# Two layers of a sequence model on one core: the Wo product in one piece, another order of the first loads, new costs in the planner, a longer ring of weights

## The chip, the cores and the metric

The kernel runs on one core of a Trainium2 chip. A core has five engines that work side by side, each with its own queue of instructions that it takes strictly in order: TensorE (PE in the profile; its weight loads are listed apart as PEld), VectorE (DVE), ScalarE (ACT), GpSimd (POOL) and SyncE (SP), which here issues transfers only. Engines wait for each other by semaphores. Transfers (DMA) run on 16 DMA engines; a queue of SP, ACT or POOL starts them. The metric is the device time of one execution in microseconds (us), lower is better; it is given as the median of several executions.

## What is computed

Two layers over 2 sequences of 1024 tokens with 512 features, all in float32. Each sub-layer is followed by a residual sum and a layer norm ("post-norm"). Cut to what matters:

```
x = layernorm(x + attn(x))        # A: q,k,v = silu(x Wq), silu(x Wk), silu(x Wv), 16 heads of 32
                                  #    chunks of 128 tokens: scores = (q k^T) * D, state S carried on with decay
                                  #    o = rms_norm_per_head(o * sigmoid(x Wg1 Wg2)) * w ;  out = o Wo
x = layernorm(x + ffn0(x))        # F: h = silu(x W1^T) * (x W3^T) ; out = hadamard(h) W2^T, 2048 wide
x = layernorm(x + scan(x))        # S: delta = softplus(...); h_t = exp(delta A) h_{t-1} + (delta x) B_t
                                  #    y = sum over 32 states of h_t C_t, + x D
x = layernorm(x + ffn1(x))        # f: h = silu(x Wg^T) * (x Wu^T) ; out = h Wd^T, 2048 wide
```

The Hadamard transform is applied to W2 once, at the start, instead of to the hidden values.

## The kernel before

**Groups and phases.** The tokens are cut into five groups (line 38): group 0 has the first two chunks of 128 tokens of the first sequence, group 1 four chunks of the second, group 2 four of the first, group 3 the last four of the second, group 4 the last two of the first. Each group g goes through V (values), A (attention), F (first feed-forward), the scan, and f (second feed-forward). `PHASES` (line 41) lists them in the order V0 A0 V1 A1 F0 F1 V2 A2 f0 F2 V3 A3 a1 F3 V4 A4 b1 F4 f2 f3 f4. Four of them are fillers (line 43): F0, f0, and the halves a1 and b1 of f1. Their matmuls have no hurry and are there to be put between the short, dependent steps of the attention of another group: F0 beside A1, f0 beside A2, a1 beside A3, b1 beside A4. The scan of a group runs on ACT (exponentials), POOL (products and sums) and DVE (the scan itself) beside the matmuls of later phases.

**The planner.** The order of instructions isn't written out by hand. Each step is an `Op` (line 68) with an engine, an estimated cost in us, a priority, the buffers that it reads, writes, takes and frees. `Order.run` (line 163) plays the whole program against these costs while the kernel is built: of the ops whose inputs are there, each engine's best is the one that can start at once, by priority, else the one that can start first; the earliest of these is put. The order in which ops are put is the order in which the engines execute them, so costs decide the order, not the time. `begin` (line 105) says when an op can start: the engine is free, inputs are written, and buffers of a named kind (`tags`) are free. With `spare` an op starts only if one buffer more than it needs is free; the fillers f0, a1 and b1 use it for their first matmuls (lines 1057 and 1108).

**Costs.** `mm_us`, `dve`, `act` and `pool` (lines 269 to 282) give a cost from the number of columns; some ops have their own (the moments of a norm at 555, `scaled` at 944, the state scan at 1436).

**Accumulators.** Matmuls write to four banks of 128x512 float32 with the tag `mm` (line 233). Every product takes one, a score step takes two at once (line 838), and the bank is free again when DVE or ACT has read it.

**Attention.** `attention` (line 612) runs the projections, then for each block of heads: transposed and decayed keys, state updates, gate, scores (two pairs of heads), outputs, then `gated`, a norm over each head (`norm`, 923) and `scaled` (938), after which the block's `normed` is set. `mixes` (981) is the product with Wo. A chunk takes four matmuls into one bank: the first two need only the first half of the blocks, the last two the second half. The list on line 984 puts the first halves of chunks 0 and 1 ahead, so that two banks are held from then until the last blocks are normed. `mixed` adds the residual and the norm, `turn` (507) transposes the result for F.

**Weights.** `load_weights` (346) streams pieces of 128x512 (256 KB) on SP through a ring of 12 buffers (`RING`, line 34), in the order of `PLAN`. At the start it holds after 4 pieces (wv) until two of the four quarters of W2 are issued, and after 12 (wq, wk) until all four are. `transformed_w2` (1138) loads the quarters (1 MB each); `butterflies` (DVE) and `w2_products` (PE, ACT) transform them and store them. `load_first` (408) loads the identity, the tokens of group 0 and the 64 KB Hadamard matrix. `load_others` (378) loads the tokens of later groups, those of group 1 at once. `load_consts` (421) loads the small tensors that the gate and the decays need.

**Scan sums.** `sums` (1464) adds the 64 partial results of a scan, every other one by an accumulating DMA. The four transposes per chunk that follow (`outputs`, 1499) are planned 6 us after the last sum (line 1493), to leave time for the last of these transfers.

Of the kernel before, what the change touches and what calls it, by code (L numbers as in the profile page):

```python
# [30 lines left out]
)  # L31


RING = 12
DB = 5
HPB = P // HD

# [41 lines left out]
class Order:  # L79
# [22 lines left out]
    def spawn(self, gen, prio=0):  # L102
        self.new.append([gen, prio, None])

    def begin(self, op):

        t = self.free[op.eng]
        for b in op.r:
            if b.written is None:
                return None  # L110
            t = max(t, b.written + self.HOP)
        for b in op.w:
            t = max(t, b.last + self.HOP)
        for name in {name for name, _ in op.a}:
            n, _, bufs = self.tags[name]
            k = sum(name == v for v, _ in op.a) + op.spare - (n - len(bufs))
            if k > 0:
                free = sorted(b.last for b in bufs if b.refs <= 0)
                if len(free) < k:
                    return None  # L120
                t = max(t, free[k - 1] + self.HOP)
        return t
# [40 lines left out]
    def run(self):  # L163
        while True:
            while self.new:
                th = self.new.pop(0)
                if self.advance(th):
                    self.threads.append(th)
            best = {}
            moved = False  # L170
            for th in list(self.threads):
                op = th[2]
                if not isinstance(op, Op):
                    if op():
                        moved = True
                        if not self.advance(th):
                            self.threads.remove(th)
                    continue
                t = self.begin(op)
                if t is None:  # L180
                    continue
                prio = op.prio + th[1]
                wrong = self.switches(op)
                now = t <= self.free[op.eng]
                key = (0, prio, wrong, t) if now else (1, t, prio, wrong)
                if op.eng not in best or key < best[op.eng][0]:
                    best[op.eng] = (key, t, th)
            if moved or self.new:
                continue
            if not best:  # L190
                assert not self.threads, [
                    (th[0].__name__, getattr(th[2], "eng", None)) for th in self.threads
                ]
                return
            _, t, th = min(best.values(), key=lambda v: v[1])
            self.put(th[2], t)
            if not self.advance(th):
                self.threads.remove(th)
# [3 lines left out]
def two_layers(  # L202
# [64 lines left out]


    def mm_us(n, cols):
        return n * max(cols * 4 / 2400 + 0.006, 0.28 if cols <= P else 0)  # L270

    def pe(us, fn, **kw):
        return Op("PE", us, fn, **kw)

    def dve(cols, fn, **kw):
        return Op("DVE", 0.145 + cols * 1.05e-3, fn, **kw)

    def act(cols, fn, **kw):
        return Op("ACT", 0.18 + cols * 0.81e-3, fn, **kw)

    def pool(cols, fn, **kw):
        return Op("POOL", 0.15 + cols * 2.25e-3, fn, **kw)

    def dma(nbytes, dst, src, eng="SP", **kw):
        of = {"SP": nc.sync, "ACT": nc.scalar, "POOL": nc.gpsimd}[eng]
# [59 lines left out]

    def load_weights():
        for i, (src, b, needs) in enumerate(pieces):
            if i in (EB, 3 * EB):
                Pools.w = i
                yield lambda: Pools.w2 >= i // EB // 3 * 2 + 2  # L350
            yield dma(
                KB256, lambda: b.t if len(src.shape) == 2 else b.t.rearrange(
                    "p (k c) -> p k c", k=2
                ), lambda: src, a=[("w", b)], r=needs,
            )
# [22 lines left out]
    def load_others():  # L378
        for gi in range(1, len(GROUPS)):
            yield gate_before(max(PHASES.index(f"V{gi}") - 1, 0))  # L380
            yield from load_x(gi)

    cst = cp.tile([P, 2 * P + 5], F32, name="cst")
# [24 lines left out]
    def load_first():  # L408
        nc.vector.memset(one, 1.0)
        nc.vector.memset(eps, EPS)  # L410
        nc.vector.memset(eps4, 4.0 * EPS)
        yield dma(KB256 / 4, lambda: ident, lambda: consts[:, C_ID : C_ID + P], w=[ident_b])
        yield from load_x(0)
        yield dma(
            65536, lambda: early[:, 0, :], lambda: consts[:, C_H : C_H + P], w=[hadamard_b]
        )
        spawn(load_weights())
        spawn(transformed_w2())
        spawn(load_consts())
# [112 lines left out]
    def normalized(gi, c, stage, store=None):  # L532

        xb = xn[gi, c]
        mv = sm.tile([P, nc.vector.BN_AGGR_DIM], F32, name="mv")
        rstd = sm.tile([P, 1], F32, name="rstd")
        neg = sm.tile([P, 1], F32, name="neg")
        nmr = sm.tile([P, 1], F32, name="nmr")
        stats = sm.tile([P, nc.vector.BN_STATS_DIM], F32, name="stats")
        s = Buf()  # L540

        def moments():
            nc.vector.bn_stats(stats, xb.t)
            nc.vector.bn_aggr(mv, stats)
            nc.vector.tensor_scalar_mul(neg, mv[:, 0:1], -1.0)

        def scales():
            log_tables()
            nc.scalar.activation(rstd, mv[:, 1:2], AF.Ln, bias=eps)
            nc.scalar.activation(rstd, rstd, AF.Exp, scale=-0.5)  # L550
            nc.scalar.activation(nmr, neg, AF.Copy, scale=rstd)
            nc.scalar.activation(xb.t, xb.t, AF.Identity, bias=nmr, scale=rstd)

        urgent = -2 if store is None else 0.2
        yield Op("DVE", 0.95, moments, w=[xb, s], prio=urgent)
        yield Op(
            "ACT", 1.6, scales, r=[s],
            w=[xb] if store is not None else [xb, there[gi, c, stage]], table=LOG, prio=urgent,
        )
        if store is not None:  # L560
            r0 = store + c * P
            yield dma(
                KB256, lambda: out[r0 : r0 + P, :], lambda: xb.t, eng="ACT", r=[xb], free=[xb]
            )
# [47 lines left out]
    def attention(gi, nxt, prio):  # L612
# [95 lines left out]
        def block(vb):  # L708
# [211 lines left out]
            def norm():  # L920
# [15 lines left out]
                def scaled():  # L936
# [4 lines left out]
                        )  # L941

                yield Op(
                    "DVE", 0.2 * S + 0.55, scaled, r=[sg, oT.whole], w=[parts[vb]], free=[sg]
                )
                normed[vb].written = parts[vb].written

# [31 lines left out]
            attended.add(gi)  # L979

        def mixes():
            accs = {}
            half = VB // 2
            for c, k in [(0, 0), (1, 0), (0, 1), (1, 1), (2, 0), (2, 1), (3, 0), (3, 1)][: 2 * n]:
                if True:
                    def mm(k=k, c=c):
                        for k_ in range(2 * k, 2 * k + 2):
                            nc.tensor.matmul(  # L988
                                accs[c].t, oT.t[:, k_, c * P : (c + 1) * P], w_o[k_].t,
                                start=k_ == 0, stop=k_ == EB - 1,  # L990
                            )

                    need = [oT.whole] + normed[k * half : (k + 1) * half]
                    ws = w_o[2 * k : 2 * k + 2]
                    if k == 0:
                        accs[c] = Buf()
                    yield pe(
                        mm_us(2, 512), mm, r=need + ws, a=[] if k else [("mm", accs[c])],
                        w=[accs[c]] if k else [],
                        free=(ws + ([oT.whole] if k else [])) if c == n - 1 else [],  # L1000
                    )
                if k:
                    spawn(mixed(c, accs[c]))

        def mixed(c, bank):
            xb = xn[gi, c]
# [14 lines left out]
    def ffn(ph, xT, store, prio=0):  # L1021
# [5 lines left out]
        for fh, nt in enumerate(parts):  # L1027
# [65 lines left out]
            def sums_of(c, f0):  # L1093
# [10 lines left out]
                if f0 == 0:  # L1104
                    accs[c] = Buf()
                yield pe(
                    mm_us(4, 512), mm, r=hs + ws, a=[] if f0 else [("mm", accs[c])],
                    spare=ph in FILLERS and ph != "F0" and f0 == 0,
                    w=[accs[c]] if f0 else [], free=hs + ws if c == n - 1 else [],
                )  # L1110

# [26 lines left out]
    def transformed_w2():  # L1138
        for dq in range(4):
            f, b = Buf(), Buf()  # L1140
            cols = slice(dq * q_d, (dq + 1) * q_d)
            if dq == 2:
                yield lambda: Pools.w >= 3 * EB
            yield dma(
                4 * KB256, lambda: f.t, lambda: w2t[:, cols].rearrange("(c p) d -> p c d", p=P),
                a=[("w2f", f)],
# [56 lines left out]
    class Scan:  # L1203
# [83 lines left out]
        def softplus(self, k, bank, u):  # L1287
# [11 lines left out]
            def logs():  # L1299
# [11 lines left out]
                prio=late,  # L1311
            )
            yield dve(
                T, lambda: nc.vector.tensor_add(r.t[:, :T], a.t[:, :T], r.t[:, :T]),
                r=[a], w=[r], free=[a], prio=late,
            )
            yield dma(
# [75 lines left out]
        def decays(self):  # L1393
# [3 lines left out]
            for i, (n, k0) in enumerate(self.units):  # L1397
                da, delta = self.da[i], self.delta[k0 // self.W]
                for j in range(self.W):
                    def exp():  # L1400
# [3 lines left out]
                            scale=a_s[:, k0 + j, n : n + 1],  # L1404
                        )

                    yield act(
                        self.T, exp, r=[delta, scan_b] + ([da] if j else []),
                        a=[] if j else [("da", da)],
                        free=[delta] if i + len(self.delta) >= U and j == self.W - 1 else [],  # L1410
                        table=EXP,
# [6 lines left out]
        def steps(self):  # L1418
# [3 lines left out]
            for i, (n, k0) in enumerate(units):  # L1422
                da, db, cs = self.da[i], self.db[i], self.cs[i // 2]
                d = lambda: da.t.rearrange("p a (r t) -> p (a r) t", r=self.R)
                for j in range(self.W):
                    def scan():
# [6 lines left out]
                        )  # L1433

                    yield Op(
                        "DVE", 0.145 + T * 2.15e-3, scan, r=[self.dec[i, j], db, da],
                        w=[self.scanned[i]], prio=1,
                    )
                if not ends(gi):
# [24 lines left out]
        def sums(self):  # L1464
# [25 lines left out]
                    r=[ys[1]], w=[ys[0]], free=[ys[1]],  # L1490
                )

            self.summed.written = max(y.written for y in ys) + 6.0
            self.done = True
            spawn(self.outputs())

# [153 lines left out]
```

## Time and profile before

| What | Value |
|---|---|
| Device time, median of 3 (lowest to highest) | 1854.84 us (1851.3 to 1860.04) |
| The profiled execution: its time, and the span from its first to its last instruction | 1854.81 us, 1853.0 us |
| PE busy | 1778.2 us, 96% |
| DVE busy | 1313.0 us, 71% |
| ACT busy | 1148.7 us, 62% |
| POOL busy | 1070.0 us, 58% |
| Mean granted TensorE clock | 0.985 of full speed |
| One 128x128 by 128x512 float32 product, shown as two records | 0.858 us start to start in a dense stretch (8 records in 3.43 us) |

"Busy" of an engine is the time in which it had an instruction; a low clock makes PE look busy for longer. So what is lost on PE is its idle time and, beside it, the time in which the granted clock was below 1. In a table by windows each row is a stretch of the span: its length, the busy us (and instructions) of each engine, the granted clock, the share of the DMA engines and GB/s. In a timeline a row is a run of equal instructions: start, length, engine, line, what it writes and reads, count, and in brackets the idle time before it and what ended that.

### The profile page before, as it was taken

The page shows a single profiled execution, that of the slowest core. Times are in us where ns is not written, and L with a number is a line of the kernel's source. Part 1 is how long each engine was busy: PE and PEld are TensorE (multiplying, and loading weights), DVE is VectorE, ACT ScalarE, POOL GpSimd, SP SyncE. Part 2 cuts the span into 40 slices and gives each one's busy share as a digit, 9 for nine tenths or more (in the row PEclk, how much of TensorE's full clock was granted, in tenths as well). Part 3 has the DMA queues.
Part 4 walks back from the last instruction along what each step waited for, and adds up shares of the span by engine and source line. Part 5 has one row for each costly group of instructions (what it writes and reads, how often), then busy time and mean ns, then how long its engine had stood idle before and what let it go on. Part 6 is the DMA issues. An engine that isn't in the chain of part 4 may idle for free.

```text
span 1853.0 us, 21250 instructions
## 1 busy us (share of the span) xinstructions
PE 1778.2 (96%) x7064; PEld 1006.8 (54%) x7064; DVE 1313.0 (71%) x1557; ACT 1148.7 (62%) x1820; POOL 1070.0 (58%) x558
## 2 busy tenths in 40 slices
PE   7999999999979999999899999999999899999998
PEld 3557754444555744444567444577775344544574
DVE  6431138994689989923999999549998998998211
ACT  3552058687756776757677757677676858775221
POOL 0000027884487899813778989337899877786000
PEclk9999999999989999999899999999999999999999
DMA  9524455774747978725478887487998775676252
GB/s 261 180 65 129 136 161 143 192 187 122 228 103 199 266 198 229 204 91 187 116 215 247 215 221 203 118 250 226 263 257 235 186 199 170 185 179 165 74 171 84
DMA packets 227708, 336.32 MB, mean 181 GB/s; under 512 B 21264, under 2 KB 131216, under 8 KB 227600
## 3 DMA queue, kind: packets, MB, share of 16 engines
q1 hardware_dynamic: 209024, 271.53, 46.8%
q0 software_dynamic: 16272, 59.25, 17.0%
q10 hardware_dynamic: 2304, 4.20, 0.6%
q8 instruction: 56, 0.92, 0.2%
q14 instruction: 52, 0.43, 0.1%
HBM read 253.12 MB, written 22.54 MB: 149 GB/s over the span
## 4 chain that ended last, share of the span: by engine, by line
PE 73%; DVE 10%; DMA 6%; ACT 5%; issue 3%; POOL 2%; SPq 0%; DVEq 0%; POOLq 0%; ACTq 0%
PE mm L1043 37%; PE mm L1097 20%; PE mm L645 5%; DVE da L1430 5%; DMA y<-dbu 3%; PE mm L594 2%; PE mm L988 2%; POOL dbu L1382 1%; ACT da L1402 1%; PE mm L832 1%; PE mm L514 1%; DVE dbu L1443 1%; DMA w<-in_wgut_dram 1%; PE mm L1244 1%; ACT L488 1%
## 5 line engine op out<-in xcount | busy, mean ns | idle before, releaser
L1382 POOL TENSOR_TENSOR dbu<-du,B 128x1024 f32<-128x1024 f32 x256 | 651.7, 2558 | 149.4 <-DMA y<-dbu 108.9
L1043 PE MATMUL mm<-xT,w 128*128 128x512 f32 (+1 forms) x1912 | 667.9, 510 | 3.6 <-DVE h L1074 1.7
L1043 PEld LDWEIGHTS mm<-xT,w 128*128 128x128 f32 x1912 | 363.3, 190 | 307.5 <-issue 269.6
L1402 ACT ACTIVATE da<-delta,a_s 128x512 f32<-128x512 f32 (+1 forms) x640 | 384.5, 605 | 148.2 <-DVE dbu L1443 121.5
L1430 DVE TENSOR_TENSOR_SCAN da<-da,hlast,dbu 128x512 f32<-128x512 f32 (+1 forms) x384 | 425.7, 1109 | 37.2 <-ACT da L1402 21.3
L1479 POOL TENSOR_TENSOR y<-y,dbu 128x1024 f32<-128x1024 f32 x123 | 323.1, 2627 | 49.7 <-DVE dbu L1443 42.9
L1097 PE MATMUL mm<-w,h 128*128 128x512 f32 x768 | 337.7, 595 | 7.5 <-DVE h L1074 4.5
L1443 DVE TENSOR_TENSOR dbu<-da,C 128x1024 f32<-128x1024 f32 x256 | 312.9, 1222 | 13.8 <-ACT hlast L1455 6.8
L1430 DVE TENSOR_TENSOR_SCAN da<-da,dbu 128x256 f32<-128x256 f32 (+1 forms) x256 | 245.9, 961 | 20.3 <-ACT da L1402 11.0
L1097 PEld LDWEIGHTS mm<-w,h 128*128 128x128 f32 x768 | 145.0, 191 | 181.9 <-issue 166.6
L1043 PE MATMUL mm<-xf,w 128*128 128x256 f32 x1024 | 230.3, 384 | 3.8 <-ACT hf L488 2.1
L1043 PEld LDWEIGHTS mm<-xf,w 128*128 128x128 f32 x1024 | 195.2, 192 | 39.3 <-issue 4.8
L488 ACT ACT_TABLE_LOAD x141 | 180.9, 1283 | 9.0 <-PE mm L645 3.8
L488 ACT ACTIVATE h<-mm 128x512 f32<-128x512 f32 x144 | 85.8, 597 | 128.9 <-PE mm L1043 64.9
L1402 ACT ACT_TABLE_LOAD x107 | 137.3, 1283 | 1.9
L1074 DVE TENSOR_TENSOR h<-h,mm 128x512 f32<-128x512 f32 x96 | 65.2, 679 | 90.3 <-PE mm L1043 84.5
L1455 ACT COPY hlast<-da 128x2 f32<-128x2 f32 (+1 forms) x160 | 25.4, 158 | 165.7 <-DVE dbu L1443 146.5
L735 POOL TENSOR_TENSOR qd<-h,q_dec 128x512 f32<-128x512 f32 x14 | 18.2, 1297 | 184.1 <-ACT h L488 118.6
L645 PE MATMUL mm<-xT,w 128*128 128x512 f32 (+1 forms) x320 | 118.3, 519 | 5.2 <-DVE sc L850 2.9
L288 POOL DMA_DIRECT2D y<-dbu x113 | 109.3, 967 | 11.5 <-DMA y<-dbu 6.6
L1116 DVE TENSOR_TENSOR xn<-mm,xn 128x512 f32<-128x512 f32 x60 | 41.0, 683 | 105.2 <-PE mm L1097 105.2
L1097 PE MATMUL mm<-w,hf 128*128 128x512 f32 x256 | 112.2, 592 | 0.0
(95 smaller groups left out, 1356.7 us busy)
## 6 DMA issues: line engine op xcount, KB each, us to landing
y<-dbu POOLq DMA_DIRECT2D x113, 512.0 KB, 6.2
w<-in_wgut_dram SPq DMA_DIRECT2D x192, 256.0 KB, 4.5
B<-rows SPq DMA_DIRECT2D x128, 256.0 KB, 4.6
C<-rows SPq DMA_DIRECT2D x128, 256.0 KB, 4.5
w<-in_wdnt_dram SPq DMA_DIRECT2D x96, 256.0 KB, 4.8
w<-in_w1t_dram SPq DMA_DIRECT2D x80, 256.0 KB, 4.4
w<-in_w3t_dram SPq DMA_DIRECT2D x80, 256.0 KB, 5.1
w<-w2h SPq DMA_DIRECT2D x80, 256.0 KB, 4.6
```

Of the source, the lines that this page charges most:

```text
L288: return Op(eng, us, lambda: of.dma_start(dst(), src(), **more), dma=nbytes, **kw)
L488: nc.scalar.activation(dst, src, AF.Silu)
L645: nc.tensor.matmul(bank.t[:, s * T : (s + 1) * T], w_qk[j][k].t[:, eb * P : (eb + 1) * P], xT.t[:, k, :], start=k == 0, stop=k == EB - 1,)
L1043: nc.tensor.matmul(bank.t[:, s * T + c0 * P : s * T + c1 * P], blocks[fb // 2][j][k // 2].t[:, k % 2 * 2 * P + k0 : k % 2 * 2 * P + k0 + P ...
L1074: 512, lambda: nc.vector.tensor_mul(t.t, t.t, pu.t), r=[pu], w=[t], free=[pu]
L1097: nc.tensor.matmul(accs[c].t, hT[f // S].t[:, s * T + c * P : s * T + (c + 1) * P], w_d[f].t, start=f == 0, stop=f == nt * S - 1,)
L1116: nc.vector.tensor_add(xb.t, bank.t, xb.t)
L1382: 1024, lambda: nc.gpsimd.tensor_mul(self.wide(self.db[i]), self.wide(du), self.row(self.bs, i)),
L1402: nc.scalar.activation(d[:, j, :], self.wide(delta)[:, j, :], AF.Exp, scale=a_s[:, k0 + j, n : n + 1],)
L1430: nc.vector.tensor_tensor_scan(d()[:, j, :], d()[:, j, :], self.wide(db)[:, j, :], init, ALU.mult, ALU.add,)
L1443: 1024, lambda: nc.vector.tensor_mul(self.wide(db), d(), self.row(self.cs, i)),
L1479: 1024, lambda: nc.gpsimd.tensor_add(y.t, y.t, db[i].t), r=o, w=[y],
```

## The change

It has seven parts.

- `mixes`: one op per chunk with all four matmuls, after every block is normed. No bank is held by a half product.
- The planner: if the best op for PE can't start, or starts more than 1 us later than a filler's first op could without its spare buffer, that filler op is put in its place.
- Later sums of a feed-forward's second product (`sums_of`, f0 > 0) get priority -1.
- The first loads: 8 pieces of weights (wv, wq) go ahead of the first two quarters of W2, the Hadamard matrix goes between these, wk follows, then the other two quarters; tokens of group 1 come only after the fourth.
- Costs of matmuls, DVE, POOL, the exponentials, the state scan, `moments`, `scaled` and the sum in `softplus`.
- The ring has 14 pieces.
- The transposes of the scan's sums are planned 10 us after the last sum instead of 6.

```diff
-RING = 12
+RING = 14
...
-    def begin(self, op):
+    def begin(self, op, spare=True):
...
-            k = sum(name == v for v, _ in op.a) + op.spare - (n - len(bufs))
+            k = sum(name == v for v, _ in op.a) + (op.spare if spare else 0) - (n - len(bufs))
...
                 t = self.begin(op)
+                if op.spare:
+                    t0 = self.begin(op, False)
+                    if t0 is not None and (last is None or t0 < last[1]):
+                        last = None, t0, th
...
+            if last and ("PE" not in best or best["PE"][1] > last[1] + 1.0):
+                best["PE"] = last
...
-        return n * max(cols * 4 / 2400 + 0.006, 0.28 if cols <= P else 0)
+        return n * max(cols * 1.68e-3 + 0.012, 0.28 if cols <= P else 0)
...
-        return Op("DVE", 0.145 + cols * 1.05e-3, fn, **kw)
+        return Op("DVE", 0.075 + cols * 1.05e-3, fn, **kw)
...
-        return Op("POOL", 0.15 + cols * 2.25e-3, fn, **kw)
+        return Op("POOL", 0.2 + cols * 2.3e-3, fn, **kw)
...
-            if i in (EB, 3 * EB):
+            if i in (2 * EB, 3 * EB):
...
             yield gate_before(max(PHASES.index(f"V{gi}") - 1, 0))
+            yield lambda: Pools.w2 == 4
             yield from load_x(gi)
...
-        yield Op("DVE", 0.95, moments, w=[xb, s], prio=urgent)
+        yield Op("DVE", 1.02, moments, w=[xb, s], prio=urgent)
...
-                    "DVE", 0.2 * S + 0.55, scaled, r=[sg, oT.whole], w=[parts[vb]], free=[sg]
+                    "DVE", 0.3 * S + 1.02, scaled, r=[sg, oT.whole], w=[parts[vb]], free=[sg]
...
-            for c, k in [(0, 0), (1, 0), (0, 1), (1, 1), (2, 0), (2, 1), (3, 0), (3, 1)][: 2 * n]:
...
+            for c in range(n):
+                acc = Buf()
+
+                def mm():
+                    for k in range(EB):
+                        nc.tensor.matmul(
+                            acc.t, oT.t[:, k, c * P : (c + 1) * P], w_o[k].t,
+                            start=k == 0, stop=k == EB - 1,
+                        )
+
+                yield pe(
+                    mm_us(EB, 512), mm, r=[oT.whole] + normed + w_o, a=[("mm", acc)],
+                    free=w_o + [oT.whole] if c == n - 1 else [],
+                )
+                spawn(mixed(c, acc))
...
-                    spare=ph in FILLERS and ph != "F0" and f0 == 0,
+                    spare=ph in FILLERS and ph != "F0" and f0 == 0, prio=-1 if f0 else 0,
...
-            if dq == 2:
-                yield lambda: Pools.w >= 3 * EB
+            yield lambda: Pools.w >= (2 + dq // 2) * EB
+            if dq == 1:
+                yield dma(
+                    65536, lambda: early[:, 0, :], lambda: consts[:, C_H : C_H + P],
+                    w=[hadamard_b],
+                )
...
-                T, lambda: nc.vector.tensor_add(r.t[:, :T], a.t[:, :T], r.t[:, :T]),
+                T + 300, lambda: nc.vector.tensor_add(r.t[:, :T], a.t[:, :T], r.t[:, :T]),
...
-                    yield act(
-                        self.T, exp, r=[delta, scan_b] + ([da] if j else []),
+                    yield Op(
+                        "ACT", 0.265 + self.T * 0.83e-3, exp, r=[delta, scan_b] + ([da] if j else []),
...
-                        "DVE", 0.145 + T * 2.15e-3, scan, r=[self.dec[i, j], db, da],
+                        "DVE", (0.2 if begins(gi) else 0.26) + T * 2.07e-3, scan, r=[self.dec[i, j], db, da],
...
-            self.summed.written = max(y.written for y in ys) + 6.0
+            self.summed.written = max(y.written for y in ys) + 10.0
```

More of the change, by code (lines that the diff above doesn't have):

```diff
@@ L169, in run @@
             best = {}
+            last = None
             moved = False
@@ L413, in load_first @@
         yield from load_x(0)
-        yield dma(
-            65536, lambda: early[:, 0, :], lambda: consts[:, C_H : C_H + P], w=[hadamard_b]
-        )
         spawn(load_weights())
@@ L981, in mixes @@
         def mixes():
-            accs = {}
-            half = VB // 2
-            for c, k in [(0, 0), (1, 0), (0, 1), (1, 1), (2, 0), (2, 1), (3, 0), (3, 1)][: 2 * n]:
[L985 to L1003, printed above, removed]
+            for c in range(n):
[11 more added lines that the diff above has]
+                spawn(mixed(c, acc))
         def mixed(c, bank):
```

## The prediction, made before the changed kernel was run

> **What bounds the kernel now.** First the busy shares and the forty slices, then a table by windows, then PE's own timeline where the windows show a loss.
>
> ```profile
> span 1853.0 us, 21250 instructions
> ...
> PE 1778.2 (96%) x7064; PEld 1006.8 (54%) x7064; DVE 1313.0 (71%) x1557; ACT 1148.7 (62%) x1820; POOL 1070.0 (58%) x558
> ```
>
> PE is the bound: the change can't take its work away, only its idle time, 1853.0 - 1778.2 = 74.8 us, and the time added by a low clock, about (1 - 0.985) x 1853 = 28 us. So the most to be had is some 100 us, less both ends. The windows say where it lies:
>
> ```profile
> core 0: us, PE busy (x) PEld busy (x) DVE busy (x) ACT busy (x) POOL busy (x), PEclk, DMA share, GB/s
> 0.00:46.30 46.30, 32.80 (x102) 18.28 (x102) 30.08 (x31) 16.30 (x32) 0.20 (x4) 0.96 0.92 261
> ...
> 270.00:480.00 210.00, 210.00 (x550) 98.16 (x549) 151.88 (x209) 163.59 (x285) 140.13 (x72) 1.00 0.61 166
> 480.00:578.00 98.00, 83.00 (x699) 53.47 (x698) 87.56 (x107) 62.80 (x101) 69.04 (x36) 0.90 0.60 170
> ...
> 860.00:940.00 80.00, 73.91 (x603) 47.20 (x602) 67.75 (x84) 54.09 (x87) 53.46 (x28) 0.94 0.59 171
> ...
> 1125.00:1230.00 105.00, 99.80 (x456) 57.73 (x455) 62.49 (x91) 77.83 (x126) 54.21 (x31) 0.98 0.63 181
> ```
>
> Feed-forward stretches lose nothing (270 to 480: 210.00 of 210). The start loses 13.5 us. A2 (480 to 578) loses 15.0 idle and 0.10 x 98 = 9.8 by its clock, A3 (860 to 940) 6.1 and 4.8, A4 (1125 to 1230) 5.2 and 2.1. Two smaller spots are 1440 to 1485 (7.4 idle, 1.8 clock) and 1545 to 1572 (4.6, 3.5); the last 34 us, a tail that stays, lose 6.5. PE's rows in A2 show the kind of loss:
>
> ```profile
> 520.28 3.60 PE L988 MATMUL mm<-w,xT 128*128 128x512 f32 x8
> ...
> 531.82 1.96 PE L923 MATMUL mm<-sg,cst 128*128 128x512 f32 x2 [2.23 <-DVE sc L850]
> 533.72 2.92 PE L832 MATMUL mm<-h 32*128 32x128 f32 x16
> 539.18 0.65 PE L878 MATMUL mm<-qd,last 32*32 32x128 f32 x8 [2.55 <-DVE sc L850]
> ...
> 549.22 3.72 PE L1043 MATMUL mm<-xf,w 128*128 128x256 f32 x16 [2.08 <-ACT hf L488]
> 552.78 1.02 PE L988 MATMUL mm<-w,xT 128*128 128x512 f32 x2
> 558.10 6.25 PE L988 MATMUL mm<-w,xT 128*128 128x512 f32 x10 [4.30 <-DVE xT L938]
> ```
>
> The eight records at 520.28 are the first halves of chunks 0 and 1 of the Wo product. Their banks are held until the second halves at 552.78 and later: for over 32 us the scores (two banks a step), the outputs and the filler share the other two. PE waits for DVE to empty a score bank, and no filler can stand in. In A1 the first halves run at 152.07 and the second at 251.29, and the two score pairs of the last block (L832, 194 and 241) are 47 us apart.
>
> **Part by part.**
>
> *Wo in one piece, and the filler without its spare.* No instruction is added: 64 products of 0.858 us stay. What is held between the halves goes. In A2 the idle gaps between 520 and 553 are 0.28 + 0.34 + 2.23 + 2.55 + 2.08 = 7.5; the 5 us windows from 530 to 545 grant 0.69, 0.50, 0.79, which costs 5 x (0.31 + 0.50 + 0.21) = 5.1: 12.6. In A3 (889.0 to 919.6): 1.33 + 0.54 + 0.16 + 1.41 + 1.23 + 0.55 = 5.2, and 0.55, 0.50, 0.92 from 900 to 915 cost 5.2: 10.4. In A1: 0.37 + 0.58 + 0.35 + 1.20, and 2.16 + 0.30 before F1, 5.0, and 1.7 of clock: 6.7. Together 29.7. Bounds: nothing, and all of it; I take two thirds, -19.8, since a bank is needed but DVE, busy 87.6 of 98 us, must still make the scores. The price of the edit: 4 products, 3.43 us, in each of A1, A2 and A3 move behind the last `normed` (1.72 in A4, with two chunks: two first halves). I cost it at nothing, for the filler takes their old place: when A2 ends at 578, 96 of the 256 products' records of f0 are done, so 160 x 0.215 = 34 us are left, in A3 half of a1. Without that cover it is 3 x 3.43 + 1.72 = 12 us. The filler that runs without its spare can hold a bank that a score needs; PE is busy meanwhile, so the price is lateness of the attention, taken up in the slow rival.
>
> [...]
>
> *First loads.* Four tokens' loads (SP, 1.85 us to issue, 1 MB) leave their place ahead of wv, four of wq (1 MB) come ahead of W2; the first quarter of W2 has as many bytes ahead as before.
>
> ```profile
> 4.46 1.94 PE L514 MATMUL mm<-cst,xn 128*128 128x128 f32 x8 [4.46 <-DMA xn<-in_x_dram]
> 9.93 8.67 PE L594 MATMUL mm<-w,xT 128*128 128x512 f32 x16 [3.53 <-DMA w<-in_wv_dram]
> 19.85 7.82 PE L645 MATMUL mm<-xT,w 128*128 128x256 f32 x32 [1.25 <-DMA w<-in_wq_dram]
> ...
> 33.04 7.08 PE L1178 MATMUL mm<-w2f,early 128*128 128x512 f32 x12 [3.16 <-DVE w2f L1159]
> 40.06 0.64 PE L664 MATMUL mm<-xT,wg 128*32 128x256 f32 x8
> ```
>
> V0 can start about 1 MB / 300 GB/s = 3.4 us earlier. But what follows keeps its time: the W2 products wait for DVE's butterflies (3.16), and the gate at 40.06, with the q and k of the second blocks behind it in the same thread, needs the small constants, issued after all of W2 until 36.6 and landed by 38.5 (2.3 after issue). Ahead of these now stand the tokens as before and two more pieces of Wo (the ring has 14): 0.5 MB at 261 GB/s is 2.0 later, 1.5 of it free. The Hadamard matrix is needed first at 27.5. Bounds -3.4 and +2.0; I take +0.5, since PE's idle time only moves to before 40.
>
> *Ring of 14.* PE's waits for a weights transfer are 0.8 + 0.2 outside the start: 0 to -1.0, I take -0.5. On SP's queue weights stand earlier, ahead of B and C rows; these land in 4.6 us, and DVE shows no wait for them.
>
> *Transposes of sums.* At 1552 PE waits 3.78 for POOL's last sum (y, L1479), and 1550 to 1560 grants 0.75 and 0.57, 3.4 more. Four us later covers 3.78. Bounds 0 and -7.2, I take -5. The lateness is behind filler or f2 products, and f4 has 34 us in hand: it begins at 1739.6, while f3 still has products to run until about 1774.
>
> *Priority of later sums.* The same products in another order: 0.
>
> *New costs.* The exponentials are the largest error of the old ones:
>
> ```profile
> L1402 ACT ACTIVATE da<-delta,a_s 128x512 f32<-128x512 f32 x384 | 262.6, 689 | 106.5 <-DVE dbu L1443 91.2 <-DVE da L1430 8.2 <-ACT hlast L1455 0.3
> ...
> L938 DVE SCALAR_TENSOR_TENSOR xT<-xT,nw,sg x20: 476/752/2720, 72.3 to 1246.7; 128x512 f32<-128x512 f32 x12, 128x256 f32<-128x256 f32 x8
> ```
>
> The plan has 0.595 for 0.689, and 0.387 for 0.477 at 256 columns: 384 x 0.094 + 256 x 0.090 = 59 us of ACT unknown to it; the new costs give 0.690 and 0.477. A scan unit of a later group, two scans and a product, takes 2 x 1.286 + 1.222 = 3.79; old 3.71, new 3.79. Single DVE steps of the attention go the wrong way, from 0.683 to 0.613 where rows have 0.68. What better costs could take is the rest of the losses: 4.3 (578 to 860), 7.3 (A4), 9.2 (1440 to 1485), so -20.8; what a new order may bring is at worst like the part of A2's 24.8 outside the hold, +12.2. I take +4, half of what A4 loses, the phase in which banks were held least.
>
> The L938 row (min, median, max in ns) is the 4.30 wait of A2: 2.37 there. [...]
>
> *Sum:* -19.8 + 0.5 - 0.5 - 5 + 4 = -20.8. Span 1853.0 - 20.8 = 1832.2; that execution took 1854.81, 1.8 more than its span, and lies on the median, 1854.84. **Forecast 1834.** Its own range: all gains and no new stalls, -29.7 - 3.4 - 1.0 - 7.2 = -41, 1813; a third of the banks' gain (-10), no gain from sums, +2 and +12, 1859.
>
> **Rivals.** *DVE falls behind (slower).* On DVE the attention's steps stand between scans, in order. If in A2 to A4 (10 blocks) scans come ahead of key decay or scores because the new costs make attention steps too cheap, or a filler's bank delays the scores, each such step waits one scan more, 1.29 idle, and 1.29 x 5.1/7.5 = 0.88 of clock: 2.17. One per block is 21.7 and eats the gain: from there on it decides. Two per block: 43 - 21 = +22, 1877. For it: DVE is busy 87.6 of 98 in A2. Against: unit costs now fit, and freed banks let filler run.
>
> *Banks weren't it (no change).* The fillers lacked something else in 528 to 550, such as their hidden tiles or weights. Then only sums, start, ring and new stalls count: -5 + 0.5 - 0.5 + 4 = -1, 1854. Against it: the wait at 549.22 is for ACT to empty the filler's own bank.
>
> *Everything fits (much faster).* Costs also clear A4 and 1440 to 1485: -41 - 16 = 1798. [...]
>
> **Chances.** Forecast 0.56, DVE behind 0.26, no change 0.12, everything 0.06. With 0.5% (9 us) as what a measurement of this kernel can tell from none: faster, below 1845.6, 0.56 + 0.06 = 0.62; same 0.12 (the forecast's own upper end is counted here); slower 0.26. The likeliest's own range is 1813 to 1859; to leave out no more than 2 in 10 the range is 1812 to 1869, which takes in the slow rival up to about one and two thirds scans per block.
>
> **What would show it.** Between A2's first scores and its Wo product PE has no gap over 2 us and the clock stays near 1; L988 comes as 32 records in a run; A1's last two score pairs stand together; V0 starts near 6.5 and the gate still near 40; no wait of L1508 for POOL. Wrong if L832 or L878 waits for `sc` are as many with four banks free, or if PE is idle after 1774 for the last scan.

## The result and the profile after

The changed kernel takes 1834.26 us (median of 4, 1830.15 to 1840.09) against 1856.78 us for the kernel before in the same comparison (4 runs, 1851.3 to 1860.04): a ratio of 0.9884, 95% interval 0.9846 to 0.9922. The forecast was 1834 us. Its profiled execution took 1835.09 us with a span of 1833.1, 19.9 us below the span before. The first lines of its page:

```profile
span 1833.1 us, 21290 instructions
...
PE 1771.5 (97%) x7064; PEld 1001.6 (55%) x7064; DVE 1311.0 (72%) x1557; ACT 1162.0 (63%) x1830; POOL 1070.7 (58%) x558
```

PE does the same 7064 records and is still the bound. Of the 19.9 us, 6.7 are shorter busy time (mostly the better clock, 0.988 for 0.985), the rest is idle time that is gone. Line numbers have moved a little: the Wo product is now L994, the scores L838, the norm over each head L929. The table by windows of the changed kernel, cut at the same phases, which end earlier now:

```profile
core 0: us, PE busy (x) PEld busy (x) DVE busy (x) ACT busy (x) POOL busy (x), PEclk, DMA share, GB/s
0.00:46.30 46.30, 31.87 (x99) 17.38 (x100) 29.89 (x30) 15.29 (x28) 0.20 (x4) 0.96 0.94 272
...
480.00:575.00 95.00, 93.47 (x721) 61.08 (x722) 81.31 (x104) 68.43 (x114) 61.30 (x31) 0.98 0.63 187
...
640.00:675.00 35.00, 30.04 (x67) 12.94 (x66) 30.91 (x30) 27.93 (x40) 29.71 (x16) 0.95 0.72 181
...
860.00:905.00 45.00, 40.41 (x418) 28.21 (x415) 40.66 (x48) 34.56 (x49) 33.95 (x18) 0.96 0.56 166
...
1545.00:1572.00 27.00, 27.00 (x84) 14.36 (x83) 26.20 (x41) 22.10 (x44) 22.14 (x11) 1.00 0.38 110
```

Read as before, idle time plus the part of the window that the clock took (length times 1 - clock), the two tables give this account. It adds up to the spans within 2 us.

| Where | Lost before, us | Lost after, us |
|---|---|---|
| Start (0 to 46.3) | 15.4 | 16.3 |
| A0, V1, A1 (46.3 to 270) | 12.1 | 2.5 |
| F1, V2 (270 to 480) | 0.0 | 8.6 |
| A2 (480 to 578; after: 575) | 24.8 | 3.4 |
| F2, V3 (to 860) | 4.3 | 15.5 |
| A3 (860 to 940; after: 905) | 10.9 | 6.4 |
| F3 (to 1125) | 0.2 | 3.6 |
| V4, A4 (1125 to 1230) | 7.3 | 8.4 |
| 1230 to 1440 | 2.1 | 2.5 |
| 1440 to 1485 (after: 1475) | 9.2 | 9.3 |
| Transposes of sums (1545 to 1572) | 8.1 | 0.0 |
| Last 34 us | 8.2 | 7.7 |
| Sum | 102.6 | 84.2 |

A1, A2, A3 and the transposes give 43.6 us; some 26 come back elsewhere, most of it in stretches that had lost next to nothing (F1 and V2, F2 and V3, F3: 4.5 before, 27.7 after). PE's timeline at the end of A2 after the change shows why A2 is quiet now:

```profile
517.83 1.16 PE L838 MATMUL mm<-h 32*128 32x128 f32 x16
...
520.72 1.43 PE L838 MATMUL mm<-h 32*128 32x128 f32 x16 [0.68 <-ACT sg L771]
522.08 3.72 PE L1043 MATMUL mm<-xf,w 128*128 128x256 f32 x16
...
532.16 7.07 PE L1043 MATMUL mm<-xf,w 128*128 128x256 f32 x32
539.07 13.90 PE L994 MATMUL mm<-w,xT 128*128 128x512 f32 x32
```

Between the last block's steps stand runs of the filler (L1043 with xf), then the Wo product comes as 32 records in one run without a gap. The longest wait in this stretch is 0.68 us; before, it was 4.30. What came back has a new name among PE's waits (in total, times, longest):

```profile
PE mm L1043 <- DMA w<-in_w3t_dram: 9.8, 4, 5.0
```

These are the windows at 640 to 675 and 1020 to 1050. In the first, SP issues two pieces of w3 at 654.26 behind a C and a B row. That C row waited for a buffer, until a product on DVE (L1447) had read the old one at 653.35; DVE was busy from 644.35 until then, with no gap over 0.1 us. The weights landed at 659.7, 5.0 us after PE was ready for them. Before, PE waited 0.2 us in all for w3. Much of the rest are two waits of the scans' input products (L1248) for copies on ACT: at 441 (2.52 us) the copy stands behind an exponential and two rows of ACT_TABLE_LOAD (1.28 us each), at 814 (3.00 us) behind the steps of a norm (L555 to L558).

### The profile page after: what moved, and what is told of

The parts are those of the page before. It is cut to its first block, busy times and chain, and to the rows that moved or that the text cites. A ratio compares the mean times of both kernels' runs of the same rounds, so it can differ in the third digit from the quotient of the medians.

```text
span 1833.1 us, 21290 instructions
## 1 busy us (share of the span) xinstructions
PE 1771.5 (97%) x7064; PEld 1001.6 (55%) x7064; DVE 1311.0 (72%) x1557; ACT 1162.0 (63%) x1830; POOL 1070.7 (58%) x558
## 4 chain that ended last, share of the span: by engine, by line
PE 62%; DVE 11%; ACT 9%; DMA 8%; POOL 5%; issue 4%; SPq 0%; DVEq 0%; ACTq 0%; POOLq 0%
PE mm L1043 29%; PE mm L1097 18%; DVE da L1434 6%; DMA y<-dbu 5%; PE mm L651 5%; POOL dbu L1386 2%; PE mm L994 2%; DVE dbu L1447 2%; ACT da L1406 2%; ACT L494 2%; POOL y L1483 1%; ACT L1406 1%; DMA w<-in_w3t_dram 1%; PE mm L838 1%; PE mm L600 1%
## 5 line engine op out<-in xcount | busy, mean ns | idle before, releaser
L1386 POOL TENSOR_TENSOR dbu<-du,B 128x1024 f32<-128x1024 f32 x256 | 644.2, 2533 | 132.7 <-DMA y<-dbu 94.3
L1043 PE MATMUL mm<-xT,w 128*128 128x512 f32 (+1 forms) x1912 | 668.8, 510 | 10.2 <-DMA w<-in_w3t_dram 9.8
L1043 PEld LDWEIGHTS mm<-xT,w 128*128 128x128 f32 x1912 | 362.7, 190 | 314.2 <-issue 267.6
L1483 POOL TENSOR_TENSOR y<-y,dbu 128x1024 f32<-128x1024 f32 x123 | 314.5, 2557 | 53.2 <-DVE dbu L1447 53.2
L1447 DVE TENSOR_TENSOR dbu<-da,C 128x1024 f32<-128x1024 f32 x256 | 312.8, 1222 | 13.5 <-ACT hlast L1459 6.9
L1043 PE MATMUL mm<-xf,w 128*128 128x256 f32 x1024 | 230.5, 384 | 0.3 <-DVE sc L856 0.3
L1043 PEld LDWEIGHTS mm<-xf,w 128*128 128x128 f32 x1024 | 195.2, 192 | 34.4 <-issue 4.9
```

The source lines that it names most:

```text
L1043: nc.tensor.matmul(bank.t[:, s * T + c0 * P : s * T + c1 * P], blocks[fb // 2][j][k // 2].t[:, k % 2 * 2 * P + k0 : k % 2 * 2 * P + k0 + P ...
L1386: 1024, lambda: nc.gpsimd.tensor_mul(self.wide(self.db[i]), self.wide(du), self.row(self.bs, i)),
L1447: 1024, lambda: nc.vector.tensor_mul(self.wide(db), d(), self.row(self.cs, i)),
L1483: 1024, lambda: nc.gpsimd.tensor_add(y.t, y.t, db[i].t), r=o, w=[y],
```

## The experiments

Each ran beside the kernel before on the same chip. Ratios are to that kernel's runs in the same comparison (its medians were 1852.4 to 1854.1 us). Kernels of different comparisons are set side by side by their medians; by their ratios such a difference comes out up to 4 us otherwise.

### One part alone, and the hold by itself

**The Wo product in one piece, alone.** The kernel before, with `mixes` of the change and nothing else:

```diff
-            for c, k in [(0, 0), (1, 0), (0, 1), (1, 1), (2, 0), (2, 1), (3, 0), (3, 1)][: 2 * n]:
...
+            for c in range(n):
+                acc = Buf()
...
+                    for k in range(EB):
```

> The kernel before with one part of the change alone: the Wo product in one piece per chunk, so that no bank is held by a half product. Banks theory: the losses of A1, A2 and A3 (idle and clock, 12.1 + 24.8 + 10.9 = 47.8 us before, 12.3 after the change) go by at least half, 1828 to 1842 us, and L988 (the Wo product) comes in one run of 32 records in A1 and A2. Rival, the costs and the filler without its spare made the gain: 1848 to 1863 us, with gaps of over 2 us left in A2.

Measured: 1821.41 us, ratio 0.9819 (0.9803 to 0.9835), 7 us below the expected range. It beats the whole change by some 13 us. A1 loses 2.9 us (46 to 270), A2 5.4 (470 to 575), A3 4.1 (840 to 900), together 12.4 against 47.8 before. The Wo products of A1 and A2 in its timeline:

```profile
173.26 13.90 PE L988 MATMUL mm<-w,xT 128*128 128x512 f32 x32
...
538.32 13.90 PE L988 MATMUL mm<-w,xT 128*128 128x512 f32 x32
```

In A1 the product ends at 187 instead of 262. The edit that moves 3.43 us of matmuls behind the last norm costs nothing, as its place is filled.

**The filler without its spare, alone.** The kernel before, with:

```diff
+            if last and ("PE" not in best or best["PE"][1] > last[1] + 1.0):
+                best["PE"] = last
```

> The kernel before with one part alone: a filler's first op may go without its spare bank when PE would wait over 1 us in the plan. Banks theory: two banks are still held in A1 to A3, so that it helps little, 1843 to 1858 us. Rival (this part made the gain): 1828 to 1842 us, with A2's loss under 8 us.

Measured: 1859.12 us, ratio 1.0024 (1.0012 to 1.0037): no gain, and 1 us outside the range on the slow side. That there is little to lend with two banks held fits this; it wasn't tested by itself.

**The halves back in the changed kernel.**

```diff
-            for c in range(n):
-                acc = Buf()
...
+            for c, k in [(0, 0), (1, 0), (0, 1), (1, 1), (2, 0), (2, 1), (3, 0), (3, 1)][: 2 * n]:
```

> The changed kernel with the Wo product in halves again (first halves of chunks 0 and 1 as soon as half the blocks are normed), all else as changed. Banks theory: A1, A2, A3 lose again, 15 to 35 us more in all, 1848 to 1868 us. Rival: within 9 us of the changed kernel, 1825 to 1843 us.

Measured: 1874.78 us, ratio 1.0111 (1.0084 to 1.0137), 7 us above the expected range. With everything else as changed, the kernel is slower than the one before the change.

**The hold without the early matmuls.** The one-piece product, but the two banks are taken when half the blocks are normed, by a planned step that issues no instruction:

```diff
+            held = [Buf() for _ in range(2)]
+            yield pe(
+                0.01, lambda: None, r=[oT.whole] + normed[: VB // 2],
+                a=[("mm", acc) for acc in held],
+            )
             for c in range(n):
-                acc = Buf()
+                acc = held[c] if c < 2 else Buf()
```

> The changed kernel, its Wo product in one piece, but the banks of chunks 0 and 1 are taken as soon as half the blocks are normed and stand empty until the product: the hold without the early matmuls. Banks theory: as with the halves, 1848 to 1868 us, with the loss in A1 to A3. Rival, that the place of the matmuls or the tail behind the last norm matters and not the banks: within 9 us of the changed kernel, 1825 to 1843 us.

Measured: 1861.51 us, ratio 1.0037 (1.002 to 1.0053), inside the range of the banks theory. This is the cleanest of the four: same matmuls in the same pieces, only two banks stand empty, and the kernel is 27 us slower than the changed one. PE's timeline in A1 of this kernel shows how:

```profile
188.72 27.79 PE L1049 MATMUL mm<-xf,w 128*128 128x256 f32 x128
216.35 13.90 PE L1103 MATMUL mm<-w,hf 128*128 128x512 f32 x32
...
230.61 1.16 PE L838 MATMUL mm<-h 32*128 32x128 f32 x16
...
243.45 2.08 PE L838 MATMUL mm<-h 32*128 32x128 f32 x16
...
249.45 2.51 PE L893 MATMUL mm<-sc,h 128*32 128x128 f32 x28 [1.91 <-DVE sc L856]
253.40 2.07 PE L929 MATMUL mm<-sg,cst 128*128 128x512 f32 x2 [1.44 <-ACT sg L919]
255.26 14.96 PE L999 MATMUL mm<-w,xT 128*128 128x512 f32 x32
```

A score needs two banks at once. The planner puts the op that can start at once, and a filler's op needs only one bank. So while the filler runs through the other two banks, the last block's two score pairs (230.61 and 243.45) wait until the whole filler is used up; in the changed kernel they run at 152.65 and 154.79. Then the rest of the attention runs bare, with waits between its steps and a low clock (0.67 granted from 225 to 250; 2.08 for a score pair that takes 1.16). A2 (575 to 650) and A3 (975 to 1025) end the same way: 8.2 and 14.7 us idle, clocks of 0.91 and 0.80.

### The other parts, each undone in the changed kernel

Since one part alone was better than all seven, the others, or the order that they make, had to cost some 13 us together.

**All costs as before** (the lines of the diff, back). 

> The changed kernel with all of its costs as before (matmuls, DVE, POOL, exponentials, state scan, moments, scaled, softplus sum). One part alone, the Wo product in one piece, gave 1821.4 us, so the other parts together cost some 13 us. Theory C, the new costs do: 1815 to 1829 us, and PE's waits for w3 weights (9.8 us after the change, 0.2 before) fall below 2 us. Rival L, the first loads, the ring or the filler without its spare do: 1830 to 1842 us.

Measured: 1834.47 us, ratio 0.9906 (0.9887 to 0.9925). The waits for w3 fall to 0.7 us, but the time doesn't: other waits take their place (4.5 us idle at 475 to 500, 4.4 at 1525 to 1550, clocks of 0.86 and 0.93). Theory C is wrong on the time, which lies in rival L's range.

**The cost of matmuls alone as before.**

```diff
-        return n * max(cols * 1.68e-3 + 0.012, 0.28 if cols <= P else 0)
+        return n * max(cols * 4 / 2400 + 0.006, 0.28 if cols <= P else 0)
```

> The changed kernel with the cost of matmuls alone as before (0.859 us for a 512 column product instead of 0.872; rows show 0.858). Theory M: with products planned 1.5% too long, PE reaches its weights earlier than the plan has them loaded; the waits for w3 weights fall below 2 us and the time to 1820 to 1830 us. Rival: another cost or part, the time stays within 1830 to 1842 us.

Measured: 1822.49 us, ratio 0.9833 (0.9807 to 0.9859), no waits for w3. Taken alone this agrees with theory M; but with the other costs also put back the 12 us are gone again, so that it isn't shown that this cost is the cause.

**The first loads as before** (order, Hadamard matrix and tokens of group 1, the lines of the diff back). 

> The changed kernel with the first loads as before (wv, then half of W2, wq, wk; tokens of group 1 at once; the Hadamard matrix ahead of the weights). By the prediction's term (+0.5, bounds -3.4 and +2.0 for the change) the time stays within 3 us of the changed kernel's, 1831 to 1837 us, V0 starts again near 9.9 us, the gate near 40. Rival, the first loads hold most of the 13 us: 1820 to 1828 us.

Measured: 1833.08 us, ratio 0.9899 (0.9877 to 0.9922), within 3 us of the changed kernel as the term said. V0 starts at 9.13, but the gate runs at 43.58 and not near 40: with the old order of loads it is as late as in the changed kernel (42.94), so that the order of loads isn't what moved it.

**Sums' transposes at 6 us.**

```diff
-            self.summed.written = max(y.written for y in ys) + 10.0
+            self.summed.written = max(y.written for y in ys) + 6.0
```

> The changed kernel with the transposes of sums planned 6 us after the last sum again. By the prediction's term (-5 for 10 us, bounds 0 and -7.2): 1834 to 1842 us, with PE waits for POOL's last sum at the transposes. Rival: what the part is worth depends on the order around it (with the Wo product in one piece alone it cost 9 us), 1822 to 1833 us.

Measured: 1844.14 us, ratio 0.9943 (0.992 to 0.9966), 10 us above the changed kernel and 2 above the range. But the cause isn't the one named. What the transposes waited for, in that kernel's rows of the line (us, times):

```profile
  DVE xn L1527: 3.0, 2
...
  POOL y L1483: 0.2, 1
```

POOL's last sum is waited for 0.2 us, not 3.8. The loss lies elsewhere: PE waits 5.4 us for w2h weights (0.5 in the changed kernel), and in A2, from 500 to 550, it is idle for 6.0 us at clocks of 0.86. Its waits for w3 weights, 8.9 us, are no more than the changed kernel's 9.8.

**Sums' transposes at 10 us, on the one-piece kernel** (the same line, the other way). 

> The kernel before with two parts, the Wo product in one piece and the transposes of sums 10 us after the last sum. Alone, the first gave 1821.4 us and shows 3.4 us of idle time between 1500 and 1525 where the transposes run. By the prediction's term for the sums (-5, bounds 0 and -7.2): 1814 to 1819 us. Rival, the order changes elsewhere and takes it back: 1820 to 1828 us.

Measured: 1830.35 us, ratio 0.9886 (0.9865 to 0.9908): 9 us slower, where the term said 5 faster, and 2 us above the rival's range too. The two runs on this part have opposite signs.

**No filler without its spare** (the two lines shown above taken out of the changed kernel). 

> The changed kernel without the filler that may go without its spare bank. Alone on the kernel before this part gave 1859 against 1853 us, no gain. Theory: with banks free it isn't needed, within 4 us of the changed kernel, 1830 to 1838 us. Rival: it fills gaps of the attention, 1839 to 1850 us.

Measured: 1818.30 us, ratio 0.9810 (0.9791 to 0.983): the fastest kernel of the study, 16 us below the changed one. Neither the theory nor the rival had this. PE's order differs first after A2's Wo product: the changed kernel puts 16 records of the filler after 8 records of transposes, this one 32 after 12. In a list of PE's runs of equal instructions some 50 of 383 rows differ in all, yet waits for w3 fall from 9.8 to 2.7 us.

**A ring of 12.**

```diff
-RING = 14
+RING = 12
```

> The changed kernel with a ring of 12 pieces. By the prediction's term (-0.5 for 14, bounds 0 and -1.0) within 2 us of the changed kernel, 1832 to 1837 us. Rival: with 14 pieces weights come early and the ring keeps the waits for w3 weights from growing, 1838 to 1850 us.

Measured: 1832.29 us, ratio 0.9880 (0.986 to 0.9901), within 2 us, as the term said. PE's waits for w3 are gone in it too, so the longer ring wasn't what kept them in check.

**A control: the order alone.** The one-piece kernel with a matmul planned 2 ns longer.

```diff
-        return n * max(cols * 4 / 2400 + 0.006, 0.28 if cols <= P else 0)
+        return n * max(cols * 4 / 2400 + 0.008, 0.28 if cols <= P else 0)
```

> The kernel before with the Wo product in one piece, and the cost of a matmul raised by 2 ns (0.859 to 0.861 us for 512 columns), which means nothing for the work: a control of how far the order alone moves the time. Theory O, single parts are worth what the order around them gives: the time moves by 3 to 15 us from 1821.4. Rival: it stays within 3 us, 1818 to 1825 us.

Measured: 1830.61 us, ratio 0.9880 (0.9856 to 0.9904). Nothing about the work has changed, some 20 of the 365 rows in the list of PE's runs of equal instructions differ, and the time moves by 9 us.

### What the runs say together

| Banks held by half a product | Kernels | Ratio to the kernel before |
|---|---|---|
| yes | before; filler without spare; hold alone; halves back | 1, 1.0024, 1.0037, 1.0111 |
| no | no filler without spare; one piece alone; old matmul cost; ring of 12; nudge; the change; one piece and sums; old loads; old costs; sums at 6 | 0.9810, 0.9819, 0.9833, 0.9880, 0.9880, 0.9884, 0.9886, 0.9899, 0.9906, 0.9943 |

The two groups don't overlap. Inside the second the scatter is 26 us, and a nudge without meaning makes 9 of them. The traces put the difference in the right place. Idle time and clock loss from the first score of an attention to the end of its Wo product, summed over A1, A2 and A3, come to 34 to 63 us in the four kernels with the hold and to 10 to 23 us in the ten without; in A1 alone to 4 to 19 us and at most 0.2. So the hold is shown to be the cause of the gain. Of the other parts only these are shown: old loads and the ring of 12 move the changed kernel by 3 us or less in this order. For the rest, an effect of under some 10 us can't be told from the order's luck by one kernel each. That the filler without its spare costs 16 us in this order stands outside the one nudge, but one nudge isn't a measure of the scatter; this stays open.

## Why the prediction was right, point by point

**The mechanism is right.** The hold of two of four banks was named as the loss in A1 to A3, and the hold put back by itself costs 27 us. L988 (now L994) comes in runs of 32, A2 has no gap over 2 us, A1's last two score pairs stand 2.1 us apart (152.65 and 154.79), and no L1512 waits for POOL. The last is a weak sign, as the runs on the sums show.

**The time is right by two errors that cancel, which is luck.** The first is in "I take two thirds, -19.8": A1, A2 and A3 gave 35.5 us in the trace and 31.5 in the run of that part alone (1852.9 to 1821.4), more than the bound of 29.7, which was called "all of it". The bound counted only waits between the two halves of a product in A1, A2 and A3. It left out what follows in A2, the 4.30 us wait and the low clock after it, and the hold of A0: its first halves run at 73.53 and 76.10, its second at 106.23, with 2.8 us of gaps between them. With free banks filler stands between the last steps of each attention, and none of them runs bare. The second is in "I take +4": new stalls came to some 26 us (F1 and V2 8.6, F2 and V3 11.2, F3 3.4, start, A4 and others the rest), above the +12.2 that was called the worst. The bound was the part of one phase, while the new order made new stalls in several.

**The cover.** Costing the move of 3.43 us at nothing was right: 160 records of f0, or 34 us, are left when A2's Wo product begins, and the product runs without a gap.

**The 4.30 wait of A2.** The sum takes nothing off for it. That was wrong for PE, right for DVE. Of the 4.30 us the DVE step was 2.37; before it PE also waited for two steps on ACT (553.82 to 555.17). After the change the step (now L944) takes 1.23 us at this place and still up to 2.571 elsewhere, but 7.07 us of filler stand ahead of the Wo product and hide the whole chain. In both traces every one of these steps that took over 1.5 us (before 2.720, 2.371 and 2.566; after 1.752, 2.527, 2.371 and 2.571) lies across a POOL product; no run shows that the product is what holds them up. The cover decides what PE sees.

**The clock.** The sum takes the clock from the windows' rows: 5.1 us in A2, 5.2 in A3, 1.7 in A1. After the change A2 and A3 are granted 0.98 and 0.96, before 0.90 and 0.94. Before, the stretch at 0.50 from 531.91 to 542.15 follows 3.41 us with 1.18 us of PE work in them. After, in A3, five gaps of 0.33 to 1.04 us lie between 886 and 892; the 3.41 us ahead of the stretch at 0.50 from 892.01 to 895.42 hold 1.73 us of work, and a norm's product in that stretch takes 2.04 instead of 1.12 us. Why the clock falls where it does wasn't tested by a run.

**The start.** Forecast +0.5, came 0.9. V0 begins at 6.02 (forecast near 6.5), the gate at 42.94 and not near 40. The small constants were issued 0.9 us later, where 2.0 was counted. What held the gate is one more W2 product ahead of it on PE (18 records instead of 16), which starts at 41.91, 0.1 us after a row of DVE's butterflies ends; the profile itself names no releaser there. As the gate is as late with the old loads, the size of this term came out near by another cause than the one counted.

**The transposes of sums.** Forecast -5, and 8.1 us are gone from that window. But with 10 us in place of 6 the changed kernel is 10 us faster and the one-piece kernel 9 us slower, and in neither of these kernels with 6 us do the transposes wait over 0.3 us for POOL's last sum. So the 3.78 us wait was a meeting in one order, not a property of the estimate.

**The rivals.** DVE falling behind wasn't seen in the attention: PE's waits for `sc` fall from 11.7 to 2.3 us. "Banks weren't it" is refuted by the hold. "Everything fits" named 1798, which no kernel reached; the best order gave 1818, and better costs weren't the reason: old and new costs give the same 1834.

## What to carry to other kernels

An accumulator that waits half done costs what it keeps others from doing. Where a step needs two buffers at once and a filler feeds on the same pool, holding two of four starves that step until the filler is used up, and then nothing covers the rest; do the sum in one go if other work can take its early half's place. In a kernel whose order comes from a planner, a small edit can reshuffle much of what follows: before a part is credited with one or two thirds of a per cent, nudge a cost by something that means nothing and see how far that moves the time. And undo parts one at a time: here the best kernels have one or six of the seven parts.

## What the runs showed of the hardware

In the traces before and after, the granted clock is 0.50 in stretches of 3.41, 6.83 or (before alone) 10.24 us (the one at the end is cut off), and 1.00 between them. One stretch at 0.50 followed 3.41 us in which PE worked for 1.18 us (before, at 531.91), another 3.41 us in which it worked for 1.73 us (after, at 892.01), with no gap longer than 2.23 and 1.04 us in them.

A DVE sum of 256 columns (L1318), 0.4 us in the least of its rows, took 5.55 us at most after the change. It ran from 1417.53 across two POOL products in a row, 2.93 and 2.92 us long.
